# Layers 1 and 3 of a four-layer graph network: the centred nodes turned by transposing transfers in place of TensorE

## The chip, the cores and the metric

The kernel runs on one core of a Trainium2 chip, in one launch. The time is the device time of an execution in microseconds (us). The engines are TensorE (PE; its weight loads, which overlap its matmuls, are shown as PEld), VectorE (DVE), ScalarE (ACT), GpSimd (POOL) and SyncE (SP), which issues transfers. Transfers (DMA) are moved by 16 DMA engines.

## The reference, cut to what matters

There are 16 graphs of 1024 nodes with 128 features each, and an integer adjacency matrix for each graph. Four layers follow each other; each normalises its input over the features, takes the positive part, mixes the nodes, and adds the result to its input:

```
h = max(layernorm(x), 0)        # every layer
layer 0: two normalised products with the softmax of the adjacency, two batch norms over all graphs
layer 1: Wh = h W^T; e = leaky_relu(s_i + t_j); alpha = softmax of e where adj != 0; x += alpha Wh
layer 2: e_k = (h * a_k) h^T for the edge's type k; softmax over the edges; x += attn h
layer 3: as layer 1 with its own weights, edges where adj > 0, and elu: x += elu(attn Wh)
```

The batch norm of layer 0 needs all graphs, so layers 1 to 3 begin when layer 0 has ended.

## The kernel before, in words

The first part (`first_layer`, `norms`) does layer 0 and takes about 360 us. A branch follows, and `plain_layers` does layers 1, 2 and 3 of one graph after the other, with up to five graphs in work at once (`"seat": [None] * 5`). The prediction is about this second part.

**Who sets the order.** The kernel doesn't issue its instructions where they are written. Each piece of work is a `step` with an engine, an assumed time in us, what it reads and writes, and the buffers ("rooms") that it holds. `Plan.attempt` simulates these steps with the assumed times: of those that can start on an engine at about the same time, the one with the lowest rank comes first. A rank is the due time of the graph (`DUES`) less the length of the chain of work that follows, with an addition for some names of steps (`URGENT`). A step with `moved` bytes is a transfer: it takes a place on one assumed wire of 300 KB per us, and lands 2.0 us after that (`RATE`, `LAND`). `Plan.emit` then issues all steps in the order that came out. So the order on each engine is fixed when the program is built; on the chip each engine works through its list and waits at each step for what the step needs.

**What a layer 1 or 3 does for one graph** (`gat`). `norm(False)` forms the statistics of the nodes on DVE (L1058, L1064), a power on GpSimd for the scale of each node (L1069, L1070), and then works in two halves of four blocks, where a block is 128 nodes by 128 features in 32-bit floats:

- `centre` (L1083) on ACT: four activations write the positive part of x minus its mean to the tile `y`, nodes on the partitions.
- `turn` (L1087) on PE: four transposes turn the four blocks, so that the features lie on the partitions. They go to one PSUM bank.
- `relu` (L1090) on ACT: copies the bank to the tile `gt`; in layers 1 and 3 it is a plain copy, since `centre` has taken the positive part.

`mix` (L1161) then multiplies each block of `gt` by the weights on PE, 16 matmul records for eight blocks, in groups of three, three and two blocks. From its results come the scores (L1166), their exponentials (L1174), a row of them for all nodes that goes through DRAM and comes back on all partitions (`send` L1187 and `fetch` L1190, on SP; in three graphs of layer 1 PE spreads it instead, L1199), the scaled values (L1217), eight weighings of 128 by 1024 on DVE (`weigh`, L1225, two inputs in SBUF), and the product on PE (L1111). The scale of the nodes is first needed after `mix`.

Layer 2 uses `norm(True)`: there `centre` runs on DVE (L1080), waits for the power, and its `turn` and `relu` on the same lines are the same instructions; this branch isn't touched. Its dots are L1257, its two exponentials L1261 and L1265, its weighings on DVE L1275, L1278 and L1293, its turned weighings on PE L1289, and its product L1111 again. The sum after each layer is L1132, L1138 and L1150; layer 3 ends with L1307 to L1319 and a store (L1327, SP). The loads of the next graphs (L995 adjacency, L998 input, L1009 layer 0's result) are on SP too.

There are four rooms for `y`, three for `gt` and eight PSUM banks.

Of the kernel before, what the change touches and what calls it, by code (L numbers as in the profile page):

```python
# [13 lines left out]
U16 = mybir.dt.uint16  # L14
# [5 lines left out]
P = 128  # L20
# [22 lines left out]
    1375.5, 1376.6, 1388.3, 1388.3,  # L43
], 0.05
DUES, WITHIN = [
    62.0, 85.5, 328.8, 104.0, 120.6, 144.4, 164.4, 185.6, 207.0, 226.0, 248.0, 269.0, 289.7, 313.6, 309.9,
    316.1,
], 0.05
L0_URGENT = {
    "<lambda>": 1.5,  # L50
# [14 lines left out]
    "turn2": -83.7,  # L65
}
URGENT = {
    "<lambda>": -18.8,
    "centre": 0.9,
    "columns": 217.6,  # L70
    "fetch": -7.9,
    "join": -33.2,
    "keep_q": 50.7,
    "larger": 0.8,
    "load_at": 60.0,
    "load_g": 11.6,
    "mask": 1.1,
    "mask_turned": 1.4,
    "power": -2.7,
    "relu": -0.6,  # L80
    "row": 3.6,
    "scaled": 111.7,
    "scores": 6.8,
    "slow": 0.7,
}
GAT_LIMIT = 30.0
DOT_KEEP = 60.0
# [17 lines left out]
class Plan:  # L105
# [11 lines left out]
    def room(self, kind):  # L117
        return Room(kind)
# [134 lines left out]
def groups_of(n, k):  # L253
    return [range(a, min(a + k, n)) for a in range(0, n, k)]
# [687 lines left out]
def plain_layers(tc, q_tiles, x, out, adj_t, gt_rows, u_rows, ident, ident_h, mhalf, gat1, gat3, edge, shift,  # L942
                 kcs, q9_all, rows9, held, kept):
    nc = tc.nc
    B, N, D = x.shape
# [6 lines left out]
    with ExitStack() as ctx:  # L952
        pool = ctx.enter_context(tc.tile_pool(name="pc", bufs=1))
# [32 lines left out]
        def batch(b):  # L986
            seat = room("seat")

            def step(engine, us_, run, reads=(), writes=(), moved=0, also=()):
                plan.step(engine, us_, run, reads, writes, moved, b, (seat, *also))  # L990
# [12 lines left out]
            X = [(xr, n) for n in range(NB)]  # L1003

            def xs(n, m=None):
                return xr.ap.rearrange("p (k d) -> p k d", d=D)[:, n if m is None else slice(n, m), :]
# [24 lines left out]
            for js in groups_of(NB, 4):  # L1031
                ps = room("ps")
# [19 lines left out]
            def norm(scaled):  # L1052
                st, mv, va, rs, y, gt = (room(k) for k in ("st", "mv", "col", "col", "y", "gt"))
                nm = None if scaled else room("col")
                for ns in TRI:
                    def stats(ns=ns):
                        for n in ns:
                            nc.vector.bn_stats(st.ap[:, n, :], xs(n))  # L1058

                    step("dve", 0.2 * len(ns), stats, [X[n] for n in ns], [(st, n) for n in ns])  # L1060

                def aggregate():
                    for n in range(NB):
                        nc.vector.bn_aggr(mv.ap[:, n, :], st.ap[:, n, :])  # L1064
                    if not scaled:
                        nc.vector.tensor_scalar_mul(nm.ap, mv.ap[:, :, 0], -1.0)  # L1066

                def power():
                    nc.gpsimd.tensor_scalar_add(va.ap, mv.ap[:, :, 1], LN_EPS)  # L1069
                    nc.gpsimd.tensor_tensor(rs.ap, va.ap, mhalf, ALU.pow)  # L1070

                step("dve", 0.7, aggregate, [(st, n) for n in range(NB)], [mv] if scaled else [mv, nm])
                step("pool", 2.1, power, [mv], [va, rs])
                for js in groups_of(NB, 4):
                    ps = room("ps")

                    def centre(js=js):
                        for n in js:
                            if scaled:
                                nc.vector.tensor_scalar(y.ap[:, n, :], xs(n), mv.ap[:, n, 0:1],  # L1080
                                                        rs.ap[:, n : n + 1], ALU.subtract, ALU.mult)
                            else:
                                nc.scalar.activation(y.ap[:, n, :], xs(n), AF.Relu, bias=nm.ap[:, n : n + 1])  # L1083

                    def turn(js=js, ps=ps):
                        for k, n in enumerate(js):
                            nc.tensor.transpose(ps.ap[:, k * P : (k + 1) * P], y.ap[:, n, :], ident)  # L1087

                    def relu(js=js, ps=ps):
                        nc.scalar.activation(gt.ap[:, js[0] * P : (js[-1] + 1) * P], ps.ap,  # L1090
                                             AF.Relu if scaled else AF.Copy)

                    if scaled:
                        step("dve", 0.84, centre, [X[n] for n in js] + [mv, rs], [(y, js[0])])
                    else:
                        step("act", 1.0, centre, [X[n] for n in js] + [nm], [(y, js[0])])
                    step("pe", 0.44, turn, [(y, js[0])], [ps], also=[gt])
                    step("act", 0.54, relu, [ps], [(gt, js[0])])
                return y, gt, rs

            def ahead(m, acc):
# [51 lines left out]

            def gat(layer, ext):
                y, gt, rs = norm(False)
                sc, ex, er, v, ub = (room(k) for k in ("tri", "tri", "col", "v", "ub"))
                parts = [room("ps") for _ in TRI]
                for ns, ps in zip(TRI, parts):
                    def mix(ns=ns, ps=ps):
                        for k, n in enumerate(ns):  # L1160
                            nc.tensor.matmul(ps.ap[:, k * WX : (k + 1) * WX], gt.ap[:, n * P : (n + 1) * P],  # L1161
                                             ext, start=True, stop=True)

                    def scores(ns=ns, ps=ps):
                        t = ps.ap[:, : len(ns) * WX].rearrange("p (k c) -> p k c", c=WX)
                        nc.vector.tensor_tensor(sc.ap[:, ns[0] : ns[-1] + 1, :], t[:, :, D:WX],  # L1166
                                                rs.ap[:, ns[0] : ns[-1] + 1].unsqueeze(2).to_broadcast([P, len(ns), 3]),
                                                ALU.mult)

                    step("pe", 0.225 * len(ns), mix, [(gt, 4 * h) for h in sorted({n // 4 for n in ns})], [ps], also=[v, sc, ex, er])  # L1170
                    step("dve", 0.17, scores, [ps, rs], [(sc, ns[0])])

                def power():
# [49 lines left out]
                for m in range(NB):  # L1223
                    def weigh(m=m):
# [5 lines left out]
                               WHOLE if layer == 3 and b == order[-1] else NB)  # L1230

            finish(gat(1, gat1))

            y, ht, _ = norm(True)
            ha, h1 = room("gt"), room("h1")

# [12 lines left out]
            for m in range(NB):  # L1249
# [3 lines left out]
                for c in chunks:  # L1253
                    ps = room("ps")
# [28 lines left out]
                for ks in groups_of(m, 4):  # L1283
                    ps = room("ps")
# [14 lines left out]
            finish(product(q, done, h1, [h1], acc))  # L1299

            acc = gat(3, gat3)
            rc, e3, r3 = room("col"), room("y"), room("y")
            for g, ns in enumerate(TRI):
                c = slice(ns[0], ns[-1] + 1)
# [529 lines left out]
```

## Time and profile before

| what | value |
|---|---|
| median of 3 runs | 1398.54 us (1398.13 to 1399.28) |
| the profiled execution: its own time | 1400.22 us |
| its span, first to last instruction | 1398.4 us |
| granted TensorE clock, mean | 0.997 |
| PE busy in the span | 1359.9 us (97%) |
| DVE busy | 1142.7 us (82%) |
| ACT busy | 824.8 us (59%) |
| POOL busy | 373.8 us (27%) |
| second part, 400 to 1398 us: PE busy of each 200 us from 500 on | 199.77, 199.52, 197.97, 197.62 |

The profile is of one execution, whose own time is 1.7 us above the median of the other runs. "Busy" is the time with an instruction of the engine under way; the records of matmuls overlap, so that the time between the starts of two, not the duration of one, is what a matmul costs in a row. L-numbers are lines of the kernel. A "chain" is followed back from the last instruction: at each step to what released it, or to the instruction before it on its engine.

### The profile page before, as it was taken

The numbers are of one execution on the slowest core, as the hardware profiler recorded it, in microseconds if no ns is written. First come the engines' busy times: TensorE is split into PE (matmuls) and PEld (weight loads), VectorE is DVE, ScalarE is ACT, GpSimd is POOL, SyncE is SP. The second block draws the span as 40 slices with busy tenths as digits, with TensorE's granted clock in tenths as the row PEclk, the third lists the DMA queues.
The fourth block names the chain that finished last, engine by engine and source line by source line (L and its number), as shares of the span: only waits on it lengthen the run. The fifth ranks groups of instructions, "written<-read, shape, count | busy, mean of one in ns | idle before, by whom it ended". The sixth has DMA issues, their size and how long they took to land.

```text
span 1398.4 us, 30562 instructions
## 1 busy us (share of the span) xinstructions
PE 1359.9 (97%) x11742; PEld 1248.6 (89%) x11742; DVE 1142.7 (82%) x3245; ACT 824.8 (59%) x2156; POOL 373.8 (27%) x458
## 2 busy tenths in 40 slices
PE   5999999999999999999999999999999999999997
PEld 3888888888998999999999999998999898998897
DVE  5899987655788888886899788887889798888886
ACT  4787888785555546645374654645474755346643
POOL 6788898552211110110011101011111111010000
PEclk9999999999999999999999999999999999999999
DMA  9999989770300002121111202122111110000001
GB/s 145 172 167 174 176 130 160 123 84 1 121 1 17 31 31 78 45 92 61 47 61 47 76 32 77 51 84 65 46 61 62 61 47 31 31 2 16 32 32 64
DMA packets 56380, 99.05 MB, mean 71 GB/s; under 512 B 6328, under 2 KB 45600, under 8 KB 52896
## 3 DMA queue, kind: packets, MB, share of 16 engines
q1 hardware_dynamic: 37504, 79.17, 16.0%
q0 software_dynamic: 18720, 17.83, 14.8%
q8 instruction: 94, 1.54, 0.5%
q14 instruction: 62, 0.51, 0.1%
HBM read 118.37 MB, written 28.95 MB: 105 GB/s over the span
## 4 chain that ended last, share of the span: by engine, by line
PE 77%; DVE 10%; issue 4%; POOL 3%; ACT 3%; DMA 3%; POOLq 0%; DVEq 0%; ACTq 0%
PE psc L1111 39%; PE psc L1257 7%; PE psa L540 7%; PE psa L625 7%; PE psc L1161 3%; PE gram L398 3%; PE psc L1289 3%; PE psc L1087 2%; DVE xg L1225 2%; PE psa L492 2%; DMA a<-in_adj_dram 2%; PE psc L1036 2%; POOL col L1070 1%; DVE y L1080 1%; DVE st L1058 1%
## 5 line engine op out<-in xcount | busy, mean ns | idle before, releaser
L1111 PE MATMUL psc<-v,xg 128*128 128x129 f32 x4096 | 482.0, 275 | 1.8 <-DVE xg L1225 1.8
L1111 PEld LDWEIGHTS psc<-v,xg 128*128 128x128 f32 x4096 | 471.7, 192 | 13.0 <-issue 7.7
L1069 POOL TENSOR_SCALAR col<-mv 128x8 f32<-128x8 f32 x48 | 22.7, 472 | 859.4 <-DVE mv L1064 757.8
L1111 PE MATMUL psc<-h,xg 128*128 128x129 f32 x2048 | 248.4, 275 | 1.0 <-DVE xg L1293 0.7
L1111 PEld LDWEIGHTS psc<-h,xg 128*128 128x128 f32 x2048 | 239.2, 192 | 10.7 <-DVE xg L1293 4.1
L1225 DVE SCALAR_TENSOR_TENSOR xg<-ub,tri,at 128x1024 f32<-128x1024 f32 x176 | 217.8, 1275 | 6.3 <-DMA at<-adj_t 3.3
L1265 ACT ACTIVATE eu<-psc,edge_shift 128x512 f32<-128x512 f32 x192 | 111.1, 591 | 142.4 <-PE psc L1257 137.7
L1257 PE MATMUL psc<-gt,gt 128*128 128x512 f32 (+3 forms) x384 | 150.7, 491 | 1.6 <-DVE xg L1293 0.5
L505 ACT ACTIVATE at<-psa 128x1024 fp8e4<-128x1024 fp8e4 x128 | 131.1, 1038 | 4.3 <-PE psa L492 4.1
L625 PE MATMUL psa<-rv,at 128*128 128x259 f16 x1024 | 122.3, 275 | 6.2 <-DVE rv L555 2.5
L1275 DVE SCALAR_TENSOR_TENSOR eu<-e,edge_shift,eu 128x1024 f32<-128x1024 f32 (+7 forms) x128 | 103.9, 811 | 29.6 <-ACT e L1261 28.9
L540 PE MATMUL psa<-hv,a 128*128 128x257 f16 x1024 | 122.9, 276 | 0.7 <-ACT at L505 0.7
L625 PEld LDWEIGHTS <-at 128*128 128x128 fp8e4 x1024 | 99.4, 98 | 23.2 <-issue 4.3
L540 PEld LDWEIGHTS <-a 128*128 128x128 fp8e4 x1024 | 100.4, 99 | 15.7 <-issue 1.1
L1083 ACT ACTIVATE y<-xg,col 128x128 f32<-128x128 f32 x256 | 78.6, 397 | 58.8 <-DVE col L1066 58.7
L1261 ACT ACTIVATE e<-psc,edge_shift 128x512 f32<-128x512 f32 x192 | 110.5, 593 | 0.0
L1225 DVE SCALAR_TENSOR_TENSOR xg<-ub,tri,atc 128x1024 f32<-128x1024 f32 x80 | 99.1, 1274 | 7.0 <-DMA atc<-adj_t 6.0
L1313 ACT ACTIVATE y<-psc,col 128x128 f32<-128x128 f32 x256 | 69.5, 421 | 55.8 <-DVE col L1307 55.8
L1138 ACT ACTIVATE y<-psc,col 128x128 f32<-128x128 f32 x256 | 72.0, 394 | 50.6 <-DVE col L1132 48.1
L552 POOL TENSOR_SCALAR rv<-r,cola 128x128 f16<-128x128 f32 x128 | 89.3, 712 | 35.7 <-DVE r L548 32.5
L1070 POOL TENSOR_TENSOR col<-col,mhalf 128x8 f32<-128x8 f32 x48 | 97.5, 2032 | 4.0
L1058 DVE BATCH_NORM_STATS2 st<-xg 128x6 f32<-128x128 f32 x384 | 82.8, 277 | 0.7
(234 smaller groups left out, 1991.3 us busy)
## 6 DMA issues: line engine op xcount, KB each, us to landing
a<-in_adj_dram POOLq DMA_DIRECT2D x128, 128.0 KB, 9.0
ub<-u_rows SPq DMA_DIRECT2D x29, 512.0 KB, 3.6
xb<-in_x_dram SPq DMA_DIRECT2D x27, 512.0 KB, 6.9
adj_t<-at SPq DMA_DIRECT2D x13, 1024.0 KB, 8.7
at<-adj_t SPq DMA_DIRECT2D x8, 1024.0 KB, 4.8
out_dram<-y SPq DMA_DIRECT2D x15, 512.0 KB, 3.4
gt_rows<-xg SPq DMA_DIRECT2D x13, 512.0 KB, 5.1
xg<-gt_rows SPq DMA_DIRECT2D x13, 512.0 KB, 4.2
```

Of the source, the lines that this page charges most:

```text
L505: nc.scalar.activation(at.ap[:, i, :], ps.ap.bitcast(F8)[:, t::2], AF.Square, saturate=False, accum_out=sums.ap[:, i : i + 1])
L540: nc.tensor.matmul(ps.ap[:, : 2 * D + 1], block[:, i % 2 :: 2], hv.ap[:, j, :], start=(j == 0), stop=(j == NB - 1))
L552: nc.gpsimd.tensor_scalar_mul(rv.ap[:, i, 0:D], r.ap[:, i, :D], rc.ap[:, i : i + 1])
L625: nc.tensor.matmul(ps.ap[:, :W2], at.ap[:, i, j * P : (j + 1) * P], rv.ap[:, i, :], start=(i == 0), stop=(i == NB - 1))
L1058: nc.vector.bn_stats(st.ap[:, n, :], xs(n))
L1070: nc.gpsimd.tensor_tensor(rs.ap, va.ap, mhalf, ALU.pow)
L1111: nc.tensor.matmul(acc[g].ap[:, k * V1 : (k + 1) * V1], weights[m].ap[:, n * P : (n + 1) * P], values.ap[:, m, :], start=(m == 0 and k == ...
L1225: nc.vector.scalar_tensor_tensor(q[m].ap, ub.ap, ex.ap[:, m, 1:2], at.ap[:, m, :], ALU.max, ALU.mult)
L1257: nc.tensor.matmul(ps.ap[:, : len(c)], ha.ap[:, m * P : (m + 1) * P], ht.ap[:, m * P + c[0] : m * P + c[-1] + 1], start=True, stop=True)
L1261: nc.scalar.activation(e.ap[:, c[0] : c[-1] + 1], ps.ap[:, : len(c)], AF.Exp, bias=shift[:, 0:1], scale=1.0 - SLOPE)
L1265: nc.scalar.activation(eu.ap[:, ROW[m] + c[0] : ROW[m] + c[-1] + 1], ps.ap[:, : len(c)], AF.Exp, bias=shift[:, 1:2], scale=SLOPE)
L1275: nc.vector.scalar_tensor_tensor(t, e.ap[:, :wide], shift[:, 2:3], t, ALU.max, ALU.mult)
```

## The change

In layers 1 and 3 the four transposes and the copy out of PSUM are replaced for each half by six steps. A 32-bit word is taken as two 16-bit words. ACT copies the lower words of the four blocks to one plane of `gt` and the upper words to another (`apart`, two copies of 128 by 512 16-bit words). SP issues two transposing transfers, one for each plane, which turn four 128 by 128 blocks of 16-bit words each and write them to `y` (`turn_words`). GpSimd copies each turned plane to every second 16-bit word of `gt` (`together`, two copies of 128 by 512), which makes 32-bit words of them again. `mix` then waits for two parts of each half. The due times and the additions to the ranks are other numbers too. The names of the numbers in a `step` are: engine, assumed us, and at the end the moved bytes; `P * N * 3` is 393216.

```diff
-    62.0, 85.5, 328.8, 104.0, 120.6, 144.4, 164.4, 185.6, ...
+    -11.2, 140.4, 376.7, 158.8, 173.7, 205.8, 213.1, 250.6, ...
 URGENT = {
...
                     if scaled:
                         step("dve", 0.84, centre, [X[n] for n in js] + [mv, rs], [(y, js[0])])
-                    else:
-                        step("act", 1.0, centre, [X[n] for n in js] + [nm], [(y, js[0])])
-                    step("pe", 0.44, turn, [(y, js[0])], [ps], also=[gt])
-                    step("act", 0.54, relu, [ps], [(gt, js[0])])
+                        step("pe", 0.44, turn, [(y, js[0])], [ps], also=[gt])
+                        step("act", 0.54, relu, [ps], [(gt, js[0])])
+                        continue
+                    step("act", 1.0, centre, [X[n] for n in js] + [nm], [(y, js[0])])
+                    c = slice(js[0] * P, (js[-1] + 1) * P)
+                    low = js[0] * P
+
+                    def plane(t, half, low=low):
+                        return t[:, low + half * 2 * P : low + (half + 1) * 2 * P].bitcast(U16)
+
+                    for half in range(2):
+                        def apart(half=half, js=js, plane=plane):
+                            nc.scalar.copy(plane(gt.ap, half).rearrange("p (k d) -> p k d", d=D),
+                                           y.ap[:, js[0] : js[-1] + 1, :].bitcast(U16)[:, :, half::2])
+
+                        step("act", 0.55, apart, [(y, js[0])], [(gt, "words", js[0], half)])
+                    for half in range(2):
+                        def turn_words(half=half, plane=plane):
+                            nc.sync.dma_start(plane(y.ap.rearrange("p k d -> p (k d)"), half).rearrange("p (k n) -> p k n", n=P),
+                                              plane(gt.ap, half), transpose=True)
+
+                        step("sp", 1.3, turn_words, [(gt, "words", js[0], k) for k in range(2)],
+                             [(y, "turned", js[0], half)], P * N * 3)
+                    for half in range(2):
+                        def together(half=half, plane=plane, c=c):
+                            nc.gpsimd.tensor_copy(gt.ap[:, c].bitcast(U16)[:, half::2],
+                                                  plane(y.ap.rearrange("p k d -> p (k d)"), half))
+
+                        step("pool", 1.5, together, [(y, "turned", js[0], k) for k in range(2)], [(gt, js[0] + half)])
...
-                    step("pe", 0.225 * len(ns), mix, [(gt, 4 * h) for h in sorted({n // 4 for n in ns})], [ps], ...)
+                    step("pe", 0.225 * len(ns), mix, [(gt, 4 * h + k) for h in sorted({n // 4 for n in ns}) for k in range(2)], [ps], ...)
```

More of the change, by code (lines that the diff above doesn't have):

```diff
@@ L45 @@
 DUES, WITHIN = [
-    62.0, 85.5, 328.8, 104.0, 120.6, 144.4, 164.4, 185.6, 207.0, 226.0, 248.0, 269.0, 289.7, 313.6, 309.9,
-    316.1,
+    -11.2, 140.4, 376.7, 158.8, 173.7, 205.8, 213.1, 250.6, 260.2, 269.1, 302.1, 328.2, 342.1, 366.5, 361.7,
+    372.4,
 ], 0.05
@@ L67 @@
 URGENT = {
[L68 to L84, printed above, removed]
+    "<lambda>": -126.0,
+    "apart": 0.4,
+    "columns": 285.1,
+    "fast": 0.8,
+    "join": -109.0,
+    "larger": -0.4,
+    "load_g": -26.0,
+    "mask": -11.1,
+    "mix": -7.9,
+    "over": 2.1,
+    "relu": 28.4,
+    "row": 169.6,
+    "scaled": 192.5,
+    "scores": 4.9,
+    "slow": 1.8,
+    "stats": 141.4,
+    "take": 17.2,
+    "together": 6.0,
+    "turn_q": 8.8,
+    "values": 32.2,
+    "weighted": -10.0,
+    "widen": 31.4,
 }
@@ L1168, in scores @@
                                                 ALU.mult)
-                    step("pe", 0.225 * len(ns), mix, [(gt, 4 * h) for h in sorted({n // 4 for n in ns})], [ps], also=[v, sc, ex, er])
+                    step("pe", 0.225 * len(ns), mix, [(gt, 4 * h + k) for h in sorted({n // 4 for n in ns}) for k in range(2)], [ps], also=[v, sc, ex, er])
                     step("dve", 0.17, scores, [ps, rs], [(sc, ns[0])])
```

## The prediction

> **What bounds the kernel now.** I read the page's busy line first, then the windows by stage, then the chain in order of time, and last the groups, transfers and timelines of the steps that the change touches.
>
> ```profile
> PE 1359.9 (97%) x11742; PEld 1248.6 (89%) x11742; DVE 1142.7 (82%) x3245; ACT 824.8 (59%) x2156; POOL 373.8 (27%) x458
> ```
>
> TensorE is busy nearly throughout. Layers 1 to 3 without their beginning and end, from the windows view (the second line's columns follow the first's names):
>
> ```profile
> core 0: us, PE busy (x) PEld busy (x) DVE busy (x) ACT busy (x) POOL busy (x), PEclk, DMA share, GB/s
> 410.00:1350.00 940.00, 933.62 (x7637) 863.40 (x7636) 798.88 (x1983) 513.52 (x1417) 108.85 (x86) 1.00 0.14 48
> ```
>
> PE stands still for 6.4 us of 940. DVE has 141 us free, ACT 426, POOL 831, and the DMA engines are used 14%. The chain in order of time (start, length, what; two places):
>
> ```profile
> 369.43 0.44 PE psc L1087 x4
> ...
> 372.59 1.79 PE psc L1161 x16
> ...
> 1348.82 0.87 PE psc L1087 x8
> ...
> 1360.52 25.92 PE psc L1111 x232
> ```
>
> It is PE's own list, one instruction after the other: four transposes are 0.44 us of it, eight are 0.87. In this stage PE work that goes away is time gained, as long as no new wait takes its place.
>
> **What is removed.** 2 layers x 16 graphs x 8 = 256 of the 384 transposes of L1087, at 0.87 / 8 = 0.109 us: **-27.9 us** of PE. With them go 64 copies of L1090, and a PSUM bank per half.
>
> **What is added, per half.** The groups by form and the transfers' issues give the nearest rows:
>
> ```profile
> L1225 DVE SCALAR_TENSOR_TENSOR xg<-ub,tri,at 128x1024 f32<-128x1024 f32 x176 | 217.8, 1275 | 6.3 <-DMA at<-adj_t 3.3 <-DMA ub<-u_rows 2.9
> ...
> L552 POOL TENSOR_SCALAR rv<-r,cola 128x128 f16<-128x128 f32 x128 | 89.3, 712 | 35.7 <-DVE r L548 32.5 <-DVE okay L598 2.0 <-DVE cola L565 0.5
> ...
> L1090 ACT ACTIVATE gt<-psc 128x512 f32<-128x512 f32 x96 | 54.3, 610 | 40.4 <-PE psc L1087 40.4
> ...
> L466 POOL TENSOR_SCALAR hv<-ya 128x1024 f16<-128x1024 f32 x15 | 43.5, 2899 | 5.1 <-DVE ya L462 5.1
> ```
>
> ```profile
> a<-in_adj_dram POOLq DMA_DIRECT2D x128, 128.0 KB, 9.0
> ...
> out_dram<-y SPq DMA_DIRECT2D x2, 128.0 KB, 3.1
> ```
>
> The last number is the median us to landing. For 4 KB a piece of the chain tells it:
>
> ```profile
> 593.01 2.03 DMA u_rows<-ur
> ```
>
> *ACT.* Two copies of 128x512 at about 0.60 us (L1090's 0.61) in place of one: 64 x 0.6 = +38 us, hidden by ACT's 426 us of idle time; what counts is 1.2 us on the path.
>
> *SP.* Two issues. Plain ones take 0.28 to 0.39 us of SP (the timelines of L1187, L1190, L1327); the order assumes 1.3. I take 0.8 each, and keep 0.3 and 1.3. `send` and `fetch` of the row and the loads are queued behind them, and behind their wait for `apart`; L1225 waited for `ub` only 3.9 us in all, so there is cover.
>
> *Landing.* No transposing transfer is in this trace. From below, the 4 KB row landed in 2.0 us; from above, 128 KB on POOL's queue took 9.0, with eight in flight. I take 3.1, the same size on the same queue, though a plain transfer.
>
> *POOL.* L466 and L552 free of contention take 2.8 and 0.6 us, so 512 elements lie near 0.6 + 384 x 2.2/896 = 1.54 us. To this comes a wait for DVE:
>
> ```profile
> L1069 POOL TENSOR_SCALAR col<-mv x48: 236/241/1332, 366.7 to 1342.6; 128x8 f32<-128x8 f32 x48
> ```
>
> (least, median, most ns). It is 0.24 us free and up to 1.33 when a weighing L1225 runs; its mean there is 0.49, L1070's 2.07 against 1.66. So a wait of 0.25 to 0.40, and 1.9 us per copy, 3.8 for two; between 1.2 (two of 0.6) and 5.2 (two of 1.54 + 1.1, the longest such wait). POOL's sum is 128 x 1.9 = 243 us beside 109: idle enough.
>
> First half centred to first `mix`: 1.2 + 1.6 + 3.1 + 3.8 = **9.7 us**; from below 1.2 + 0.6 + 2.0 + 1.2 = 5.0, from above 1.2 + 2.6 + 9.0 + 5.2 = 18.0. Before, transposes and copy took 0.44 + 0.61 = 1.1.
>
> **What hides it.** PE takes `mix` from a long list, not at once. A graph in the timelines of ACT and PE:
>
> ```profile
> 909.91 2.45 ACT L1083 ACTIVATE y<-xg,col 128x128 f32<-128x128 f32 x8 [3.09 <-DVE col L1066]
> ```
>
> ```profile
> 918.26 1.04 PE L1087 MATMUL psc<-ident,y 128*128 128x128 f32 x8
> ...
> 920.38 1.95 PE L1161 MATMUL psc<-gat,gt 128*128 128x131 f32 x16
> ```
>
> The first half is centred at 911.2, `mix` begins at 920.1: 8.9 us, of which the old path needs 1.1. I paired the n-th eight activations of L1083 with the n-th sixteen matmuls of L1161 (the names don't tell graphs apart, so some pairs may be wrong): the median is 10.1 us. The first two are 3.6 and 5.0. Of the other 30, twelve are under 9.7: 3.1, 3.7, 3.9, 4.9, 5.7, 7.0, 8.0, 8.2, 8.9, 8.9, 9.2, 9.2; they fall short by 36 us together. The order is laid out anew with the longer path and four other graphs to draw on; I let a quarter stand, **+9** (0 to 36).
>
> *The beginning.* There only three graphs are loaded and the first pair has 3.6 us: 9.7 - 3.6 = 6.1, of which I let 1 be filled: **+5** (0 to 14). At the end PE has 25.9 us of products left after the last `mix`, and the last pair 12.5 us of slack: nothing. The new due times and ranks only order the lists; they can win no more than PE's 6.4 us of standstill, and what they may lose lies in these waits.
>
> *POOL's and SP's queues.* 16 powers of layer 2 (L1069, L1070), on which DVE's L1080 waits, can now stand behind copies that wait for a landing. At worst 16 x 3.8 = 61 us; with POOL idle for two thirds of the stage, **+2** (0 to 10).
>
> *DVE held by POOL.* A layer 0 place, DVE beside POOL's L466 (two timelines):
>
> ```profile
> 48.29 2.78 POOL L466 TENSOR_SCALAR hv<-ya 128x1024 f16<-128x1024 f32 x1 [1.91 <-DVE ya L462]
> ```
>
> ```profile
> 49.08 1.33 DVE L584 TENSOR_TENSOR hl<-g,hl 128x1024 f16<-128x1024 f32 x1
> ```
>
> L584 has two inputs in SBUF, begins 0.8 us into the 2.78 and takes 1.33 instead of 1.22: it was let go 0.9 us after POOL's start, long before POOL's end. For 512 elements that is 0.45 us, met by half of the copies (L1225, L1275 and L1278 are 482 of the 940 us): 128 x 0.45 / 2 = 29 us more for DVE, 828 of 912, 91%. Between 0 and 128 x 1.54 = 197. PE lost 6 us with DVE at 85%: **+3** on the path.
>
> The Trainium skill (SBUF — State Buffer, "Who interferes with whom") says that a DVE instruction with two SBUF inputs and a GpSimd one that reads SBUF lock each other out for the whole instruction. L584's row is milder; by the page the hold would be the upper end, 197 us.
>
> The skill also speaks against the change: VectorE: DVE Perf Modes, "The three transpose paths", puts a 128x128 16-bit transpose at 1309 ns by DMA, 390 by TensorE, and advises TensorE where PSUM will do. Four blocks one after the other would then be an estimated 5.2 us per transfer and 21 per graph and layer, and the change would lose. No run here shows it.
>
> **The sum** against the profiled execution's own 1400.2 us: -27.9 + 9 + 5 + 2 + 3 = -8.9, so 1391.3; the median of runs lies 1.7 lower: **1389.6 us**.
>
> **Rivals.**
> - *All of it hidden.* Half of the pairs have 10 us and more. -27.9 with 0 to 5 at the beginning: 1371 to 1376. Against it: twelve short pairs. 13%.
> - *Slower: the landing comes late.* With 9.0 in place of 3.1 the path is 15.6, with issues of 1.3 it is 16.6; the 30 pairs then fall short by 153, a quarter is 38, the beginning costs 12, the rest 5: +27.5, or **1426**. It decides from a path of about 11.6 us, a landing of 5.0. For it: nothing in the trace shows a transposing transfer, and every engine's list is fixed with 2.0 + 1.3 us assumed. Against it: the 512 KB transfers of this stage on SP (`ub`, `out`, `xg`) land in 3.4 to 4.2 us. 29%.
> - *DVE becomes the bound.* It has 912 - 799 = 113 us, so from 0.88 us lost per copy on; at 1.54 it is 996 of 912, +84 - 27.9, about 1455. L584's row speaks against it. 9%.
> - *Gain eaten up,* a path of 11.6: about 1398. 9%.
>
> **How the numbers follow.** My forecast, 1380 to 1395, has 40%. A measurement of this kernel can tell about 0.2% (2.8 us) from no change. Faster: 40 + 13 = 53%; the same: 9%; slower: 29 + 9 = 38%. The range reaches from the whole gain, 1371, to the late landing, 1426: it leaves out the bound by DVE and a worse landing.
>
> **What would show it.** Right: L1087 down to 128 records; PE busy lower by about 28 us; landings near 3 us; POOL's copies 1.5 to 2.5 us; L1161 waiting for POOL less than 15 us in all. Wrong: landings over 5 us and PE waiting for POOL's copies tens of us; L1225 well above 1.3 us and DVE near 95%; or PE idle for a landing of the row behind SP's queue.

## The result, and the profile after

The changed kernel takes 1409.13 us (median of 4 runs, 1407.80 to 1413.17) where the kernel before took 1398.91 (4 runs, 1398.13 to 1399.67) beside it: a ratio of 1.0078, 95% interval 1.0056 to 1.0100. It is slower, by 10 us. The profiled execution took 1407.8 us, its span 1406.0, 7.6 more than before.

The page's busy line of the changed kernel, and its windows view of layers 1 to 3 without their ends, with the columns' names:

```profile
PE 1344.9 (96%) x11486; PEld 1228.8 (87%) x11486; DVE 1170.4 (83%) x3245; ACT 854.0 (61%) x2220; POOL 523.8 (37%) x586
```

```profile
core 0: us, PE busy (x) PEld busy (x) DVE busy (x) ACT busy (x) POOL busy (x), PEclk, DMA share, GB/s
410.00:1350.00 940.00, 917.49 (x7419) 843.61 (x7418) 821.86 (x1988) 541.80 (x1482) 232.45 (x195) 1.00 0.23 63
```

TensorE has 256 instructions less, but it now stands still for 22.5 of the 940 us, where it was 6.4, and gets through 7419 matmuls in them instead of 7637. VectorE does the same 3245 instructions in 27.7 us more. Of the groups by form, the weighings and the new copies:

```profile
L1255 DVE SCALAR_TENSOR_TENSOR xg<-ub,tri,at 128x1024 f32<-128x1024 f32 x176 | 223.2, 1312 | 6.9 <-DMA ub<-u_rows 4.6
...
L1125 POOL COPY gt<-y 128x512 uint16<-128x512 uint16 x128 | 152.8, 1247 | 185.0 <-DMA y<-gt 145.0
```

The two groups of weighings (`at`, shown, and `atc`) are 9.6 of VectorE's 27.7 us. Most of the rest lies in other operations with two inputs in SBUF: layer 2's weighings of L1305 take 5.6 us more, the sums of L1180 4.6.

(The changed kernel's lines: `centre` L1088, `apart` L1112, `turn_words` L1118, `together` L1125, `mix` L1191, scores L1196, exponentials L1204, weighings L1255, products L1141.)

**Where TensorE lost time.** To compare kernels that do different amounts of TensorE work I kept an account: each matmul is worth the median interval to the next start of its form in the kernel before; what an execution takes beyond the sum of these is lost (a wait, or a stretch at a lower granted clock, as the 0.50 from 388 to 389 us of the changed kernel). By stages of the span, in us:

| kernel | work | lost to 360 | 360 to 420 | 420 to 1340 | end | span |
|---|---|---|---|---|---|---|
| before | 1340.1 | 31.3 | 3.1 | 16.3 | 7.6 | 1398.4 |
| changed | 1312.2 | 31.1 | 18.9 | 34.9 | 8.9 | 1406.0 |

The work fell by 27.9 us as forecast. The beginning of the second part lost 15.8 us more, its body 18.6, the rest 1.1: -27.9 + 15.8 + 18.6 + 1.1 = +7.6.

*The beginning.* The windows view of the kernel before, then of the changed one:

```profile
380.00:400.00 20.00, 20.00 (x184) 20.00 (x182) 16.29 (x50) 11.97 (x39) 2.61 (x3) 1.00 0.01 2
400.00:420.00 20.00, 19.22 (x148) 16.74 (x147) 17.89 (x33) 10.09 (x23) 3.00 (x2) 1.00 0.00 0
```

```profile
380.00:400.00 20.00, 16.72 (x122) 16.22 (x122) 12.36 (x24) 9.66 (x27) 13.45 (x15) 0.85 0.45 93
400.00:420.00 20.00, 17.61 (x126) 15.86 (x125) 16.59 (x67) 14.24 (x43) 6.24 (x6) 0.92 0.15 40
```

184 matmuls became 122 in the first 20 us: TensorE waits, and its granted clock falls to 0.85. ScalarE's timeline, before and after, shows what comes ahead of the first graph's exponential (128x24, the last line of each; the copies on which TensorE waits below, `qt` on L1032, stand in the gap of the second):

```profile
367.43 2.44 ACT L1083 ACTIVATE y<-xg,col 128x128 f32<-128x128 f32 x8
...
371.73 2.43 ACT L1083 ACTIVATE y<-xg,col 128x128 f32<-128x128 f32 x8
...
374.96 0.22 ACT L1174 ACTIVATE tri<-tri 128x24 f32<-128x24 f32 x1
```

```profile
366.76 2.45 ACT L1088 ACTIVATE y<-xg,col 128x128 f32<-128x128 f32 x8 [1.31 <-DVE col L1071]
369.11 2.17 ACT L1112 COPY gt<-y 128x512 uint16<-128x512 uint16 x4
371.18 2.45 ACT L1088 ACTIVATE y<-xg,col 128x128 f32<-128x128 f32 x8
373.53 2.16 ACT L1112 COPY gt<-y 128x512 uint16<-128x512 uint16 x4
...
377.40 2.45 ACT L1088 ACTIVATE y<-xg,col 128x128 f32<-128x128 f32 x8
379.75 2.17 ACT L1112 COPY gt<-y 128x512 uint16<-128x512 uint16 x4
381.82 2.45 ACT L1088 ACTIVATE y<-xg,col 128x128 f32<-128x128 f32 x8
384.17 0.61 ACT L1112 COPY gt<-y 128x512 uint16<-128x512 uint16 x1
384.67 0.23 ACT L1204 ACTIVATE tri<-tri 128x24 f32<-128x24 f32 x1
```

Two graphs were centred ahead of it; now four, with thirteen copies. The exponential comes 9.7 us later. Its own place in ScalarE's list is the smaller part of that: the first graph's last scores end at 374.65 us before and at 382.60 after, so that 7.9 us come ahead of them, and the exponential then waits 2.1 us in the list, where it waited 0.3. The scores are late because the first `mix` is (it began at 372.43 us before). TensorE's timeline of the changed kernel:

```profile
376.66 0.62 PE L1046 MATMUL psc<-rows,qt 128*128 128x128 bf16 x8 [2.74 <-ACT qt L1032]
377.56 0.62 PE L1046 MATMUL psc<-rows,qt 128*128 128x128 bf16 x8 [0.29 <-ACT qt L1032]
378.79 3.54 PE L1191 MATMUL psc<-gat,gt 128*128 128x131 f32 x16 [0.60 <-POOL gt L1125]
```

Ahead of `mix` stand sums for the next graphs, whose `qt` ScalarE copies only at 375.60, behind the centring of two graphs and eight of the new copies. After that `mix` waits 0.60 us for the joins, and takes 3.54 us instead of 1.95, at a mean granted clock of 0.55 behind TensorE's wait. With the exponential the first weighings are late (VectorE's timeline, before and after):

```profile
379.28 9.65 DVE L1225 SCALAR_TENSOR_TENSOR xg<-ub,tri,at 128x1024 f32<-128x1024 f32 x8
```

```profile
389.32 11.45 DVE L1255 SCALAR_TENSOR_TENSOR xg<-ub,tri,at 128x1024 f32<-128x1024 f32 x8
```

These last two lines show the other loss too: the same eight weighings take 11.45 us instead of 9.65, with GpSimd copies beside them.

### The profile page after: what moved, and what is told of

The parts are those of the page before. It is cut to its first block, busy times and chain, and to the rows that moved or that the text cites. A ratio compares the mean times of both kernels' runs of the same rounds, so it can differ in the third digit from the quotient of the medians.

```text
span 1406.0 us, 30640 instructions
## 1 busy us (share of the span) xinstructions
PE 1344.9 (96%) x11486; PEld 1228.8 (87%) x11486; DVE 1170.4 (83%) x3245; ACT 854.0 (61%) x2220; POOL 523.8 (37%) x586
## 5 line engine op out<-in xcount | busy, mean ns | idle before, releaser
L1141 PEld LDWEIGHTS psc<-v,xg 128*128 128x128 f32 x4096 | 472.9, 192 | 17.1 <-issue 7.2
L1141 PE MATMUL psc<-v,xg 128*128 128x129 f32 x4096 | 481.6, 276 | 3.3 <-DVE xg L1255 1.9
L1141 PE MATMUL psc<-h,xg 128*128 128x129 f32 x2048 | 245.3, 275 | 0.6 <-DVE xg L1308 0.2
L1141 PEld LDWEIGHTS psc<-h,xg 128*128 128x128 f32 x2048 | 238.0, 192 | 6.1 <-issue 2.9
L1255 DVE SCALAR_TENSOR_TENSOR xg<-ub,tri,at 128x1024 f32<-128x1024 f32 x176 | 223.2, 1312 | 6.9 <-DMA ub<-u_rows 4.6
L1125 POOL COPY gt<-y 128x512 uint16<-128x512 uint16 x128 | 152.8, 1247 | 185.0 <-DMA y<-gt 145.0
L1287 PE MATMUL psc<-gt,gt 128*128 128x512 f32 (+3 forms) x384 | 147.1, 492 | 4.5 <-DVE xg L1323 1.9
L1305 DVE SCALAR_TENSOR_TENSOR eu<-e,edge_shift,eu 128x1024 f32<-128x1024 f32 (+7 forms) x128 | 109.0, 855 | 33.8 <-ACT e L1291 33.4
L1088 ACT ACTIVATE y<-xg,col 128x128 f32<-128x128 f32 x256 | 78.7, 396 | 71.4 <-DVE col L1071 57.0
L545 PEld LDWEIGHTS <-a 128*128 128x128 fp8e4 x1024 | 100.7, 99 | 15.8 <-issue 0.8
L1255 DVE SCALAR_TENSOR_TENSOR xg<-ub,tri,atc 128x1024 f32<-128x1024 f32 x80 | 103.3, 1331 | 1.8 <-DMA ub<-u_rows 1.1
L557 POOL TENSOR_SCALAR rv<-r,cola 128x128 f16<-128x128 f32 x128 | 89.1, 711 | 36.4 <-DVE r L553 33.3
```

The source lines that it names most:

```text
L545: nc.tensor.matmul(ps.ap[:, : 2 * D + 1], block[:, i % 2 :: 2], hv.ap[:, j, :], start=(j == 0), stop=(j == NB - 1))
L557: nc.gpsimd.tensor_scalar_mul(rv.ap[:, i, 0:D], r.ap[:, i, :D], rc.ap[:, i : i + 1])
L1125: nc.gpsimd.tensor_copy(gt.ap[:, c].bitcast(U16)[:, half::2], plane(y.ap.rearrange("p k d -> p (k d)"), half))
L1141: nc.tensor.matmul(acc[g].ap[:, k * V1 : (k + 1) * V1], weights[m].ap[:, n * P : (n + 1) * P], values.ap[:, m, :], start=(m == 0 and k == ...
L1255: nc.vector.scalar_tensor_tensor(q[m].ap, ub.ap, ex.ap[:, m, 1:2], at.ap[:, m, :], ALU.max, ALU.mult)
L1287: nc.tensor.matmul(ps.ap[:, : len(c)], ha.ap[:, m * P : (m + 1) * P], ht.ap[:, m * P + c[0] : m * P + c[-1] + 1], start=True, stop=True)
```

## The experiments

Three theories. **A:** the transfers' path (issue, queue on SP, landing) holds up the graphs, above all in the beginning. **B:** GpSimd's copies and VectorE's operations with two inputs in SBUF hold each other. **C:** the loss of the beginning lies in the order of the lists, which was laid out around a longer path. The x kernels keep the changed kernel's order on every engine. Ratios are to the kernel before beside them.

**x1_small_joins.** GpSimd copies 8 words instead of 512, ScalarE a contiguous plane.

```diff
-nc.scalar.copy(plane(gt.ap, half).rearrange(...), y.ap[:, js[0] : js[-1] + 1, :].bitcast(U16)[:, :, half::2])
+nc.scalar.copy(plane(gt.ap, half), plane(y.ap.rearrange("p k d -> p (k d)"), half))
-nc.gpsimd.tensor_copy(gt.ap[:, c].bitcast(U16)[:, half::2], plane(y.ap..., half))
+nc.gpsimd.tensor_copy(gt.ap[:, c].bitcast(U16)[:, ::2][:, half * 8 : half * 8 + 8], plane(y.ap..., half)[:, :8])
```

> The changed kernel (1409.1 us) with the same order on every engine; GpSimd's two copies per half take 8 words each in place of 512, so that they still wait for the transposing transfers but hardly touch SBUF (the turned values are left out of the result). Theory A, the beginning: twelve transposing issues of 1.25 us stand one behind the other on SP while only three graphs are loaded, PE idles and its clock falls; then this changes little: 1406 to 1410. Theory B, VectorE and GpSimd hold each other up (VectorE +28 us, copies of up to 6.8 us): this takes away VectorE's 28 us and the late copies, and 10 us or more of time: 1395 to 1400. Theory C, the new order itself is worse: nothing, 1409.

1389.57 us, ratio 0.9923 (0.9906 to 0.9940): 20 us faster than the changed kernel, more than B asked for. VectorE is back where it was (page):

```profile
PE 1338.1 (96%) x11486; PEld 1227.2 (88%) x11486; DVE 1141.5 (82%) x3245; ACT 853.0 (61%) x2220; POOL 449.4 (32%) x586
```

**x2_plain_transfers.** The transfers move the planes without transposing them (`transpose=True` and the rearranging taken out).

> The changed kernel with the same order; the 128 transfers move the same bytes without transposing them (the turning is left out of the result). An issue should take 0.3 us of SP in place of 1.22. Theory A: the loss at the beginning, 16 us of PE, falls by 8 to 11: 1398 to 1401. Theory B: GpSimd's copies are the same, so 1406 to 1409. Theory C: 1409.

1407.09 us, ratio 1.0049 (1.0032 to 1.0066). That they transpose costs some 2 to 4 us.

**x3_path_out.** No transfers and no joins; ScalarE copies the plane.

> The changed kernel with the same order; transfers and GpSimd's copies are left out, ScalarE's copies of the same size write the unturned words (the turning is left out of the result). This is what the change could bring if its path cost nothing at this order. Theories A and B: nearly the whole 27.9 us against the kernel before, 1371 to 1378. Theory C: clearly less, 1385 or more, since the order stays.

1387.43 us, ratio 0.9906 (0.9889 to 0.9923): 2 us from x1. With GpSimd's 512 words gone, the transfers and the short joins cost next to nothing. Yet the beginning is as bad as ever (VectorE's timeline):

```profile
388.45 9.64 DVE L1252 SCALAR_TENSOR_TENSOR xg<-ub,tri,at 128x1024 f32<-128x1024 f32 x8
```

The first weighings still start 9 us late, now in 9.64 us. There is no transfer and no join left to wait for, only the order and, in it, ScalarE's two copies per half. The first `mix` still begins late, behind the same sums (TensorE's timeline):

```profile
375.85 0.62 PE L1046 MATMUL psc<-rows,qt 128*128 128x128 bf16 x8 [2.20 <-ACT qt L1032]
...
377.54 3.34 PE L1188 MATMUL psc<-gat,gt 128*128 128x131 f32 x16
```

How much of this is ScalarE's new work, 7.1 us for the thirteen copies, and how much the two graphs drawn forward, 4.9 us of centring, no run separates.

**x4_first_three_out.** As x3, for layer 1 of the first three graphs alone.

> As the kernel with the path left out, but in layer 1 of the first three graphs alone (their turning is left out of the result); all other graphs as in the changed kernel. Theory A: the beginning's 11 us come back, 1397 to 1400. Theory B: little, 1406 to 1409. Theory C: 1409.

1408.20 us, ratio 1.0056 (1.0039 to 1.0073). Theory A falls for the beginning. The account of the four:

| kernel | work | lost to 360 | 360 to 420 | 420 to 1340 | end |
|---|---|---|---|---|---|
| x1_small_joins | 1312.2 | 30.2 | 17.3 | 19.9 | 8.3 |
| x2_plain_transfers | 1312.2 | 31.5 | 17.8 | 35.5 | 7.7 |
| x3_path_out | 1312.2 | 30.9 | 16.8 | 19.1 | 8.1 |
| x4_first_three_out | 1312.2 | 31.6 | 17.8 | 37.4 | 8.0 |

So B is the body (34.9 to 19.9, and the kernel before had 16.3), and the beginning's 17 us are in each of these, which all keep the order and ScalarE's copies.

**x6_memset.** x1, and behind each short join GpSimd writes the 512 words without reading any.

```diff
+nc.gpsimd.memset(gt.ap[:, c].bitcast(U16)[:, half::2], 0)
```

> As x1_small_joins (ScalarE's copies in a contiguous pattern, GpSimd's joins of 8 words: both leave the turned data out), with a GpSimd memset of the same 128x512 16-bit words behind each of the 128 short joins: GpSimd writes as much as in the changed kernel, and reads next to nothing. If the two engines hold each other over anything that GpSimd does in the memory: VectorE back at about 1165 to 1172, weighings beside a memset at 1.5 us and more, 1402 to 1412 us. If only GpSimd's reading holds the two-input operations: VectorE stays at 1141 to 1145, the weighings at 1.28 us, and the time at 1388 to 1393.

1388.21 us, ratio 0.9919 (0.9903 to 0.9936). GpSimd is as busy as in the changed kernel, and the weighings are not held (page, then two lines of the groups):

```profile
PE 1336.1 (96%) x11486; PEld 1225.2 (88%) x11486; DVE 1143.1 (82%) x3245; ACT 852.0 (61%) x2220; POOL 524.4 (38%) x714
```

```profile
L1126 POOL MEMSET gt<- 128x512 uint16 x128 | 86.5, 676 | 38.4 <-DMA y<-gt 18.5 <-PE psc L1141 4.4 <-ACT gt L1112 3.7
```

```profile
L1255 DVE SCALAR_TENSOR_TENSOR xg<-ub,tri,at 128x1024 f32<-128x1024 f32 x176 | 216.5, 1275 | 8.6 <-DMA ub<-u_rows 5.5 <-DMA at<-adj_t 2.9
```

It is GpSimd's reading that holds the weighings: 1275 ns beside 128 memsets, 1312 beside 128 copies. The Trainium skill (SBUF — State Buffer, "Who interferes with whom") says just that: a VectorE instruction with two inputs in SBUF contends with a GpSimd instruction that reads SBUF, not with one that only writes it.

**x7_beside.** x1, and behind the second short join GpSimd copies both turned planes of `y` onto themselves: the reading is there, but beside the path.

```diff
+if half:
+    for t in words:
+        nc.gpsimd.tensor_copy(t, t)
```

> As x1_small_joins (ScalarE's copies in a contiguous pattern, GpSimd's joins of 8 words: the turned data are left out), and behind the second short join of each half GpSimd copies the two turned planes of 128x512 16-bit words onto themselves: it reads and writes as many words as in the changed kernel, beside the path instead of on it, so that no product waits for a copy that VectorE holds up. Theory B1 (the cost is VectorE's lengthened operations): VectorE's busy time at 1165 to 1175 as in the changed kernel, and the time at 1399 to 1410. Theory B2 (the cost is the lateness of the joins, held up behind VectorE's back-to-back weighings for up to 7 us): VectorE's busy time as high, and the time at 1387 to 1393. In between, both have a share.

1400.10 us, ratio 0.9997 (0.9987 to 1.0007), 10.5 us above x1. These copies are shorter (0.867 us against 1.247), and VectorE is up by 19.4 us over x1 instead of 28.9:

```profile
PE 1342.5 (96%) x11486; PEld 1227.7 (88%) x11486; DVE 1160.9 (83%) x3245; ACT 853.3 (61%) x2220; POOL 551.0 (39%) x714
```

TensorE loses 29.5 us in the body here, between x1's 19.9 and the changed kernel's 34.9. So copies beside the path cost about 0.54 us of the end per us of VectorE (10.5 / 19.4); on 28.9 that would be an estimated 16 of the 20. How much of it is VectorE's lengthened operations and how much lateness of the joins is not shown: in x7 too a short join can stand behind a long copy, and the longest record of one is 11.7 us.

**x5_act_joins.** The joins on ScalarE, in the same order.

```diff
-nc.gpsimd.tensor_copy(gt.ap[:, c].bitcast(U16)[:, half::2], ...)
+nc.scalar.copy(gt.ap[:, c].bitcast(U16)[:, half::2], ...)
```

> The changed kernel in its own order on every engine, except that the 128 joining copies (128x512 16-bit words) run on ScalarE, in place of GpSimd, at the places that the order gives them. Nothing is left out. Theory B (VectorE's two-input operations and GpSimd's copies hold each other: 16 to 18 us of the end): VectorE's busy time falls back to 1141 to 1145, ScalarE's rises by 128 x 0.6 = 77 us to about 931, and the time comes near the run with copies of 8 words: 1388 to 1398. Rival E (what costs is that a waiting join stands ahead of other work in an engine's queue: on ScalarE it would stand ahead of the exponentials and the evictions of layer 2): VectorE falls as well, but the time stays at 1403 or goes to 1420.

1416.36 us, ratio 1.0121 (1.0104 to 1.0138): slower still, although VectorE is back at 1142.6. TensorE loses 43.9 us in the body. The group of the joins:

```profile
L1125 ACT COPY gt<-y 128x512 uint16<-128x512 uint16 x128 | 98.1, 803 | 20.1 <-DMA y<-gt 19.8
```

98 us of joins, with 20 us of waiting for transfers in front of them, stand where the order left no time for them: my expectation from B alone was wrong, and the rival E held for this order.

The y and z kernels were laid out anew: due times and priorities were searched for each, in the same way.

**y1_first_by_pe.** Layer 1 of the first three graphs is turned by TensorE, the rest by transfers and GpSimd.

```diff
+if by_pe:
+    step("pe", 0.44, turn, [(y, js[0])], [ps], also=[gt])
+    step("act", 0.54, relu, [ps], [(gt, js[0]), (gt, js[0] + 1)])
+    continue
-y, gt, rs = norm(False)
+y, gt, rs = norm(False, early and layer == 1)
```

> The changed kernel, but layer 1 of the first three graphs is turned by TensorE again (24 transposes, 24 x 0.109 = 2.6 us of TensorE), and the order of the whole second part is worked out anew with due times and priorities searched for this kernel. GpSimd makes the other 116 joins. Nothing is left out. Theory C (the beginning's 16 us are lost because the order lets ScalarE prepare several graphs ahead of the first graph's exponential, to cover the long path): TensorE loses 3 to 6 us between 360 and 420 us instead of 19, and with the 2.6 us of transposes and nine tenths of VectorE's holds left the time is 1409 - 13 + 2.6 - 1.6 = 1397 (1392 to 1402). Rival (that loss belongs to something else that the short path does not touch): 1405 to 1412.

1401.86 us, ratio 1.0012 (1.0002 to 1.0021). The beginning loses 8.0 instead of 18.9, a little less of a gain than C asked for; the holds stay (VectorE 1171.3).

**y4_act_joins_anew.** y1 with the joins on ScalarE (`step("act", 0.55, together, ...)`).

> As y1_first_by_pe, and the joins run on ScalarE instead of GpSimd (116 x 0.78 = 90 us more of ScalarE), in an order worked out for that. Nothing is left out. Theory B and C together (VectorE's holds and the order of the beginning are the whole loss, and x5_act_joins was slow only because its order put the waiting joins ahead of ScalarE's evictions): VectorE at 1142, 1397 - 17 = 1380 (1375 to 1388). Rival E (a join on ScalarE costs as much as on GpSimd, wherever it stands, because it waits for a transfer in ScalarE's queue): VectorE at 1142 as well, but 1395 to 1415.

1385.92 us, ratio 0.9894 (0.9877 to 0.9910), the fastest. Its joins wait 47.7 us for transfers, more than in x5, but TensorE loses 20.1 us in the body where it lost 43.9:

```profile
L1144 ACT COPY gt<-y 128x512 uint16<-128x512 uint16 x116 | 83.5, 798 | 47.7 <-DMA y<-gt 47.7
```

So E falls: the place in the order decides what a waiting join costs.

**y5_half_and_half.** y1 with one join of each pair on ScalarE.

```diff
+copy = nc.scalar.copy if half else nc.gpsimd.tensor_copy
```

> As y1_first_by_pe, with one join of each pair on ScalarE (58) and one on GpSimd (58), in an order worked out for that. Nothing is left out. Theory B and C: VectorE's holds halved (1154 to 1158), half of 17 us less than y1_first_by_pe: 1385 to 1390. Rival E: 1393 to 1405.

1387.93 us, ratio 0.9908 (0.9891 to 0.9924), the expected time. VectorE falls further than expected, to 1146.6: why half of the copies hold it so much less than half as long was not looked into.

**z1_before_anew and z2_after_anew.** Both kernels untouched, but for due times and priorities searched anew.

> The kernel before, unchanged but for the due times and priorities of its second part, which are searched anew in the same way and about as long as those of y4_act_joins_anew. Nothing is left out. If y4_act_joins_anew is faster because its order was searched anew: about the same here, 1383 to 1389. If it is faster because TensorE has 25 us of transposes less: 1392 to 1400 here.

> The changed kernel, unchanged but for due times and priorities searched anew in the same way: all 64 turnings still go by transfers and GpSimd. Nothing is left out. If the loss of the beginning belongs to the one order that the changed kernel came with: TensorE's loss between 360 and 420 us falls from 19 to 5 us or less, VectorE stays near 1170, and the time is 1393 to 1399. If it belongs to the long path of the first graph, in whatever order: 10 us and more stay lost there, and the time is 1401 to 1409.

z1: 1388.20 us, ratio 0.9912 (0.9887 to 0.9937). z2: 1412.16 us, ratio 1.0091 (1.0068 to 1.0115). The account of those laid out anew:

| kernel | work | lost to 360 | 360 to 420 | 420 to 1340 | end |
|---|---|---|---|---|---|
| z1_before_anew | 1340.1 | 33.3 | 2.3 | 4.4 | 7.9 |
| z2_after_anew | 1312.2 | 31.3 | 18.0 | 36.3 | 8.8 |
| y1_first_by_pe | 1314.9 | 31.1 | 8.0 | 37.7 | 7.6 |
| y4_act_joins_anew | 1314.9 | 31.0 | 6.9 | 20.1 | 11.5 |
| y5_half_and_half | 1314.9 | 33.6 | 3.9 | 21.7 | 12.7 |

z2 narrows C; its time is 3 us above what the long path was expected to give. In a second order for the same steps the beginning loses 18.0 again and the body 36.3: neither belongs to one unlucky order. ScalarE's timeline shows the same picture, the fourth graph centred and taken apart ahead of the first exponential:

```profile
379.13 2.44 ACT L1098 ACTIVATE y<-xg,col 128x128 f32<-128x128 f32 x8
381.48 2.16 ACT L1122 COPY gt<-y 128x512 uint16<-128x512 uint16 x4
383.54 0.22 ACT L1214 ACTIVATE tri<-tri 128x24 f32<-128x24 f32 x1
```

With the first graphs' path short again (y1, y4, y5) the loss is 4 to 8. So the loss goes with the longer path of the first graphs, ScalarE's copies among it. x3 and x4 show that it acts through the order: with transfers and joins gone and the order kept, it stays.

z1 puts y4's gain in its place: the kernel before, with all of TensorE's transposes and only a new order, is as fast within the intervals. It loses 4.4 us in the body (windows view):

```profile
420.00:1340.00 920.00, 919.57 (x7564) 855.41 (x7563) 781.63 (x1976) 513.31 (x1430) 102.24 (x86) 1.00 0.15 49
```

Of the 15 us by which y4 is faster than the kernel before, a new order alone gives 11; that the transfers with ScalarE's joins bring the rest is not shown, since the intervals of y4 and z1 overlap.

## Why the prediction was wrong

The forecast of 1389.6 us had the sign wrong; the time lies in the range of 1371 to 1426. By its steps:

- **What is removed, -27.9:** measured -27.9, with the 128 records of `turn` left that were forecast.
- **The path of 9.7 us** was priced about right, but its parts were not. In the beginning SP's issues take 1.22 and 1.26 us (0.8 was taken), the joins start 2.6 us after the start of the second issue (3.1 for the landing), and a free copy takes 0.76 us (1.9 was taken; the mean is 1.247): 1.2 + 1.2 + 2.6 + 1.5 = 6.5 us undisturbed. As it ran, with lists and holds, a half took 7.8 to 21.8 us from its centring to the end of its second join, 11.1 in the median (the n-th half paired with the n-th two joins). The other estimate in the text, 5.2 us per transfer from the Trainium skill (VectorE: DVE Perf Modes, "The three transpose paths"), is far above the 2.6 of this trace.
- **Short pairs, +9, and the queues, +2:** at most 3.6 us together (18.6 lost in the body less the 15.0 that x1 gives back). TensorE waited for the copies themselves for only 1.9 us in all: the path was hidden far better than "a quarter" of the short pairs said.
- **The beginning, +5:** measured 15.8. This step failed in its reasoning. It priced the first pair's wait for its own path and let 1 us be filled, and said that the new due times could lose no more than lies in such waits. In fact the fill was the damage: the wait was filled with two more graphs and with ScalarE's copies, and these stood ahead of the `qt` copies that TensorE's list needs before the first `mix`, and ahead of the first exponential. Which of the two weighs more stays open.
- **DVE held by POOL, +3:** the size was right, 27.7 us against 29, and 0.45 us is the most that a weighing lost (the longest is 1.731 us, 0.45 above the free 1.276). That the product fits so well is partly luck: 84 of the 128 copies, not 64, had an operation with two inputs in SBUF (of over 0.35 us) begin beside them, so that a meeting cost about 0.33 us. What failed is the last sentence, "PE lost 6 us with DVE at 85%: +3". It took VectorE's free share as cover. x1 puts GpSimd's long copies, holds and late joins together, at 20 us of the time, and x7 gives about half a us per us.

The chain in order of time shows a place where there is no cover:

```profile
1246.41 0.68 DVE st L1063 x3
1247.09 7.31 DVE xg L1255 x5
1254.40 0.85 DVE xg L1180
...
1256.30 0.63 DVE eu L1305 x2
...
1257.63 3.74 ACT y L1343 x14
...
1261.42 0.66 PE psc L1092 x4
```

For these 15 us nothing on the chain is TensorE's. Five weighings that take 6.05 us in a row undisturbed took 7.31 on it, and the addition of 256 columns behind them 0.85, where one at 668.5 us in the same trace takes 0.41. This is one place, and the chain alone would not show the cause: it can be followed back only to 1238.45 us, and the kernel before had three pieces of 18.5 to 18.7 us without TensorE in its body. What shows it is x1, x6 and x7.

The rival that was slower, the late landing, had the sign and not the mechanism: x2 and x3 leave the transfers 2 to 4 us, and it is by luck that the range it opened up to 1426 holds the measured time. "DVE becomes the bound" named the right engine with the wrong condition: it asked for an average of 100%, and VectorE averaged 87% in the body (821.86 of 940). The signs given for "wrong" missed it too: the weighings' mean of 1.31 us is hardly above the 1.3 named there, and 87% is not near 95%; TensorE's 1.9 us of waiting for the copies was even a sign of "right".

## What to carry to other kernels

An engine at 85% is no cover for another one that it feeds in turns: price a lengthened operation by whether the next product waits for it. Here about half of it reached the end (10.5 of 19.4 us). A copy put on GpSimd because GpSimd is idle was paid by VectorE here (28.9 us over x1), since the copy reads SBUF while VectorE reads two inputs; ScalarE took the copies for 16 us less (y4 against y1) in an order laid out for it. And where a planner lays out the lists, compare kernels at orders searched in the same way: a new order alone was worth 11 us here, as much as the whole change cost.

## What the runs showed of the hardware

Holding goes both ways. In the changed kernel GpSimd's copy, 0.76 us when free, waits through a row of weighings that are not lengthened at all (GpSimd's timeline, then VectorE's):

```profile
918.38 7.15 POOL L1125 COPY gt<-y 128x512 uint16<-128x512 uint16 x2 [6.20 <-DMA y<-gt]
```

```profile
918.18 6.05 DVE L1255 SCALAR_TENSOR_TENSOR xg<-ub,tri,at 128x1024 f32<-128x1024 f32 x5
```

Its first copy started just after the first weighing and lasted 6.48 us, through all five. Elsewhere, as in the eight weighings of 11.45 us, VectorE gives way, by up to 0.45 us each. Who began first is part of the answer: all 28 weighings (of 256) that took over 1.33 us began beside a copy already under way, and none of the 12 that a copy joined later did. But 14 others with a copy under way were not lengthened, the last four of the row above among them, so what decides stays open.

Memsets, which left the weighings alone in x6, did hold layer 2's `centre` on VectorE, which has one input in SBUF. Its records without and with the memsets, x1 and x6 (the numbers are least, median and most ns):

```profile
L1085 DVE TENSOR_SCALAR y<-xg,mv,col x128: 325/340/347, 412.0 to 1255.9; 128x128 f32<-128x128 f32 x128
```

```profile
L1085 DVE TENSOR_SCALAR y<-xg,mv,col x128: 159/341/932, 411.3 to 1254.9; 128x128 f32<-128x128 f32 x128
```

Only 11 of the 128 met a memset; these took 0.74 us in the median.
